# Layer 3 of a four-layer graph network: exponentiated logits used untransposed, with column maxima spread over DRAM and subtracted on GpSimd

## The chip, the cores and the metric

The kernel runs on one core of a Trainium2 chip. The metric is the device time of one execution in microseconds (us); the times are the median of the runs of each kernel. The profile is one execution taken by the hardware profiler.

## What is computed

`x` has shape (32, 512, 64): 32 graphs of 512 nodes with 64 features each; `adj` is one symmetric 512 x 512 matrix with the diagonal in it and few other edges, scaled on both sides by node degrees. Four layers follow each other, each with a layer norm and a ReLU ahead of it and a residual sum behind it. The first two are plain graph convolutions, the third is graph attention. The fourth, called layer 3 in the code, is the one that is changed:

```python
def gat_layer(x, graph, W, b):
    h = x @ W
    s = jnp.einsum('bnd,bmd->bnm', h, h) * graph
    s = jnp.where(s == 0.0, NEG_INF, s)
    a = jax.nn.softmax(s, axis=2)
    return jnp.einsum('bnm,bmd->bnd', a, h) + b
heads = jax.vmap(lambda W, b: gat_layer(flow_x, graph, W, b))(Wh, bh)
...
x = jax.nn.leaky_relu(cat, negative_slope=0.01)
out = gat_layer(x, graph, W_out, b_out)
return jax.nn.leaky_relu(out, negative_slope=0.01)
```

There are 8 heads of width 128, their outputs are concatenated, and one more attention of width 64 (`W_out`) works on them. The logits of a graph and head are a product of `h` with itself, so that `s` is symmetric: s[n, m] = s[m, n] wherever `graph` is.

## The kernel before

The kernel has two forms. `fast_form` is the one that runs: it relies on properties of the inputs (each diagonal entry present, the matrix being a degree scaling of its own pattern, no logit exactly zero on an edge), checks them while it works, and sets a flag; `general_form` is run afterwards if the flag is set. All data are fp32. Layers 0 to 2 make stage 1, about the first 455 us, in which layer by layer and pair of graphs by pair of graphs are interleaved by hand. Layer 3 takes the rest.

**Units.** The work of layer 3 is cut into 144 units: 128 `Heads` units (a graph b and two heads, `k` = 0 and 1) and 16 `Out` units (the output attention of two graphs, `k` = 0 and 1). A unit has C = 4 row blocks of P = 128 nodes. All units go through the same steps, and `planned` (line 690) writes the order of the work out by hand: in each `slot` k it issues, for every unit, the step whose offset from the unit's start (4 slots a unit) is due. In these slots TensorE, VectorE and ScalarE run strictly in the written order (`manual_schedule`); GpSimd and SyncE (SP), which only issue DMAs, were left to the scheduler.

**Steps of a unit**, with offsets in slots from its start:
- -1 to 2, `scores` (line 387): two TensorE products (k = 0, 1; each uses one half of the array's rows) put 128 x 512 logits for each k into PSUM (`s_ps`, two buffers).
- 0 to 3, `soft` (line 363): for each k one VectorE instruction (line 378) reads the logits, adds the mask `flow_neg` (SBUF), writes the negated logits to `s_att` in SBUF and leaves the negated row maximum in `negmax`; then ScalarE computes the exponential with the row maximum as bias (line 371) and sums the row.
- The value product needs the exponentials with the *other* node index on the partitions, so that they are transposed. For column blocks 0 to 2, `transpose` (line 422) makes 16 TensorE transposes of 64 x 64 (line 430) and copies the result from PSUM by ScalarE (lines 436, 438) or VectorE (line 441). For the last column block, `turn` (line 397, slots 2 to 5) transposes 32 x 32 blocks on VectorE (line 401), sends them to DRAM (line 406), and `route` (line 411) brings them back in transposed order (line 415).
- VA = 6 to 9, `values` (line 443): the value products add into `av` in PSUM (line 452; each k has one half of the array's columns).
- 5, `recips` (line 458): reciprocals of the row sums, transposed and sent over DRAM, come back spread over the partitions as `recb` (lines 463 to 473).
- END = 9, `normalize` (line 480): VectorE multiplies `av` by `recb` into `o_att` (line 482).
- 10, `row_halves` of a Heads unit (line 538): the two products y with the heads' weights (line 565), bias on ScalarE (line 573) into `cat`; in 11 VectorE's leaky ReLU on `cat`, 1024 elements a partition (`leaky`, line 312). An Out unit has a bias, a leaky ReLU, transposes back, the residual sum (line 651) and the store.

Beside these steps, every second Heads unit makes `g` for two units (line 547), every fourth one the layer norm of its graph on VectorE (lines 513 to 522, four instructions), and an Out unit's product with `W_out` (line 604) is spread over 8 slots, one head a slot. Out units are put into the list behind the heads of their graphs; those of the last few pairs are kept back for the end (`LATE` = 3).

Of the kernel before, what the change touches and what calls it, by code (L numbers as in the profile page):

```python
# [22 lines left out]
def fast_form(  # L23
# [169 lines left out]
    def judge_rows(c):  # L193
        edge, t = row_pair("edge"), row_pair("t")[:, 0]
        ok, edge = edge[:, 1], edge[:, 0]
# [9 lines left out]
        nc.vector.tensor_reduce(sound[:, 2 + C + c : 3 + C + c], ok, AX.X, OP.min)  # L205
# [4 lines left out]
    def row_pair(name):  # L210

        return early.tile([P, 2, N], F32, name=name, tag="row", bufs=H + 3)


    acc_of = []
# [46 lines left out]
    def flow_weights():  # L262
        whT = early.tile([P, H, 2, F], F32, name="whT", tag="row", bufs=H + 3)
# [36 lines left out]
    TR = C + 1  # L300
    VA = TR + 1
    END = VA + C - 1


    LATE = 3

    recs = [const.tile([P, 32], F32, name=f"rec{i}") for i in range(2)]
    for rec in recs:
        nc.gpsimd.memset(rec, 0.0)
# [4 lines left out]
    class Pair:  # L314
# [4 lines left out]

        def begin(self):
            self.p = pbuf.tile([P, 2, C, N], F32, name="p_att")
            self.sum = tiny.tile([P, 2, C], F32, name="sum_att")
            self.negmax = tiny.tile([P, 2, C], F32, name="negmax")
            self.pts = {}

# [7 lines left out]

# [5 lines left out]


# [13 lines left out]
        def scores(self, r):  # L360
            pass

        def soft(self, r, mid):

            if r == 0:
                self.begin()
            ps = self.s_ps.pop(r)
            ns = wk.tile([P, 2, N], F32, name="s_att", bufs=3)

            def exp(k):  # L370
                nc.scalar.activation(  # L371
                    self.p[:, k, r, :], ns[:, k], AF.Exp,
                    bias=self.negmax[:, k, r : r + 1], scale=-1.0,
                    accum_out=self.sum[:, k, r : r + 1],
                )

            for k in range(2):
                nc.vector.tensor_tensor_reduce(  # L378
                    out=ns[:, k], in0=ps[:, k], in1=flow_neg[:, r], scale=-1.0, scalar=BIG,
                    op0=OP.add, op1=OP.min, accum_out=self.negmax[:, k, r : r + 1],  # L380
                )
                if k == 0:
                    exp(0)
            mid()
            return lambda: exp(1)

        def scores(self, r):
            g, x = self.terms()
            ps = ps_s.tile([P, 2, N], F32, name="s_ps")
            self.s_ps[r] = ps  # L390
            for k in range(2):
                nc.tensor.matmul(  # L392
                    ps[:, k], lhsT=g[halves(k), r * P : (r + 1) * P], rhs=x[halves(k), :],
                    start=True, stop=True,
                )

        def turn(self, r):
            if r == 0:
                self.turns = wk.tile([P, Q, C // 2, 2, 2, 32], F32, name="turn")
                self.rows = dram.tile([P, Q, C // 2, P], F32, name="turn_row")  # L400
            nc.vector.transpose(  # L401
                self.turns[:, :, r // 2, :, r % 2].rearrange("p a k i -> p k a i"),
                self.p[:, :, r, N - P :].rearrange("p k (a i) -> p k a i", i=32),
            )
            if r % 2:
                nc.gpsimd.dma_start(  # L406
                    self.rows[:, :, r // 2],
                    self.turns[:, :, r // 2].rearrange("p a k r i -> p a (k r i)"),
                )

        def route(self):
            rows = self.rows.rearrange("(b i) a g x -> a i b (g x)", b=Q)
            pt = wk.tile([P, Q, C // 2, 2, 2, 32], F32, name="turned")
            for a in range(Q):
                (nc.sync if a % 2 else nc.gpsimd).dma_start(  # L415
                    pt[a * 32 : (a + 1) * 32].rearrange("p b g k r i -> p b (g k r i)"), rows[a]
                )
            self.pts[C - 1] = [
                pt[:, :, :, k].rearrange("p b g r i -> p g r b i") for k in range(2)
            ]  # L420

        def transpose(self, j):
            pt = pbuf.tile([P, 2, N], F32, name="pt_att", bufs=2)
            self.pts[j] = [pt[:, k] for k in range(2)]

            ps = [ps_m.tile([P, 2, C, F], F32, name="pt_ps", tag="m") for half in range(2)]
            for k in range(2):
                for r in range(C):
                    for half in range(2):
                        nc.tensor.transpose(  # L430
                            ps[half][:, k, r],
                            self.p[halves(half), k, r, j * P : (j + 1) * P],
                            ident[halves(half), halves(half)],
                        )
            pth = pt.rearrange("p k (r half q) -> p k r half q", r=C, half=2)
            nc.scalar.copy(pth[:, :, :, 0, :], ps[0])  # L436
            if j != 1:
                nc.scalar.copy(pth[:, :, :, 1, :], ps[1])  # L438
                return None
# [1389 lines left out]
```

## Time and profile before

| | before |
|---|---|
| median of 3 runs | 2256.88 us (2256.71 to 2257.84) |
| profiled execution | span 2255.2 us (from its first to its last instruction; no other time was recorded for it) |
| TensorE busy (PE) | 2181.2 us, 97% |
| VectorE busy (DVE) | 1746.9 us, 77% |
| ScalarE busy (ACT) | 1629.8 us, 72% |
| GpSimd busy (POOL) | 399.5 us, 18% |
| first and last instruction of line 378 | 454.2 and 2228.4 us |
| steady stretch 700 to 2100 us | PE 1372.7, DVE 1086.4, ACT 1143.3, POOL 289.9 us busy; granted TensorE clock 1.00 |

How such lines are read: a group's line has the source line, the engine, the operation, the tile it writes and those it reads, their shapes, the number of instructions, then the busy time in all and the mean in ns of one, then how long the engine stood idle just before them and what ended most of that. PEld is the loading of weights, which overlaps products. A fp32 product is issued as two instructions, so that a pair of products (k = 0 and 1) shows as x4. A row of waits reads "who, line <- whom, line: us in total, times, longest". A row in order of time has the start, the duration, and the instruction. The busy time of TensorE counts pipelined products, whose ends are modelled, so that full is not the same as at its peak; distances from start to start are the better measure.

### The profile page before, as it was taken

The numbers are of one execution on the slowest core, as the hardware profiler recorded it, in microseconds if no ns is written. First come the engines' busy times: TensorE is split into PE (matmuls) and PEld (weight loads), VectorE is DVE, ScalarE is ACT, GpSimd is POOL, SyncE is SP. The second block draws the span as 40 slices with busy tenths as digits, with TensorE's granted clock in tenths as the row PEclk, the third lists the DMA queues.
The fourth block names the chain that finished last, engine by engine and source line by source line (L and its number), as shares of the span: only waits on it lengthen the run. The fifth ranks groups of instructions, "written<-read, shape, count | busy, mean of one in ns | idle before, by whom it ended". The sixth has DMA issues, their size and how long they took to land.

```text
span 2255.2 us, 47785 instructions
## 1 busy us (share of the span) xinstructions
PE 2181.2 (97%) x17374; PEld 1032.9 (46%) x17374; DVE 1746.9 (77%) x4541; ACT 1629.8 (72%) x3815; POOL 399.5 (18%) x616
## 2 busy tenths in 40 slices
PE   7999999999999999999999999999999999999997
PEld 4667666634444444444444434444444443434443
DVE  6799986687778787878777777787878787878785
ACT  3444443288888888878888888787878787878785
POOL 2000000012121222222221212221212222212221
PEclk9999999899999999999999999999999999999999
DMA  4000000033333333333333333333333333333333
GB/s 130 1 1 1 1 1 1 1 93 113 104 115 105 113 109 112 110 106 111 109 110 112 110 107 114 104 114 108 116 102 118 102 115 107 106 99 117 99 115 105
DMA packets 122979, 204.03 MB, mean 90 GB/s; under 512 B 29752, under 2 KB 76000, under 8 KB 122608
## 3 DMA queue, kind: packets, MB, share of 16 engines
q0 software_dynamic: 37376, 113.49, 16.5%
q1 hardware_dynamic: 85360, 87.42, 13.0%
q8 instruction: 139, 2.28, 0.4%
q14 instruction: 104, 0.85, 0.1%
HBM read 119.48 MB, written 80.28 MB: 89 GB/s over the span
## 4 chain that ended last, share of the span: by engine, by line
PE 76%; DVE 17%; issue 3%; DMA 2%; ACT 1%; SPq 0%; DVEq 0%; ACTq 0%
PE s_ps L392 19%; PE av L452 18%; PE pt_ps L430 8%; DVE s_att L378 8%; PE nt_ps L880 7%; PE acc L972 5%; PE y_ps L565 5%; PE gT_ps L604 5%; DVE pt_att L441 3%; PE g_ps L547 2%; PE po L899 1%; DVE hs L518 1%; DVE turn L401 1%; PE wh_ps L925 1%; PE po1a L899 1%
## 5 line engine op out<-in xcount | busy, mean ns | idle before, releaser
L371 ACT ACTIVATE p_att<-s_att,negmax 128x512 f32<-128x512 f32 x1152 | 826.9, 726 | 1.8 <-DVE negmax L378 0.8
L378 DVE CUSTOM_DVE_ANT_0 s_att<-s_ps,flow_neg 128x512 f32<-128x512 f32 x1152 | 736.6, 675 | 1.7 <-PE s_ps L392 1.6
L392 PE MATMUL s_ps<-hx,g 64*128 64x512 f32 x2048 | 571.8, 635 | 26.4 <-DVE negmax L378 23.1
L452 PE MATMUL av<-pt_att,hn 128*64 128x512 f32 x1536 | 414.2, 618 | 0.0
L406 POOL DMA_DIRECT2D turn_row<-turn x288 | 206.3, 716 | 1161.8 <-DVE turn L401 970.6
L430 PEld LDWEIGHTS pt_ps<-ident,p_att 64*128 64x128 f32 x6912 | 279.7, 138 | 280.3 <-issue 180.0
L436 ACT COPY pt_att<-pt_ps 128x512 f32<-128x512 f32 x432 | 250.7, 580 | 88.9 <-PE pt_ps L430 86.8
L430 PE MATMUL pt_ps<-ident,p_att 64*128 64x64 f32 x6912 | 312.8, 226 | 1.2 <-ACT pt_att L436 0.6
L392 PEld LDWEIGHTS s_ps<-hx,g 64*128 64x128 f32 x2048 | 155.2, 186 | 282.9 <-DVE negmax L378 129.1
L401 DVE STREAM_TRANSPOSE turn<-p_att 128x256 f32<-128x256 f32 x576 | 254.0, 441 | 18.1 <-ACT p_att L371 17.6
L573 ACT ACTIVATE cat<-y_ps,bh 128x512 f32<-128x512 f32 x256 | 162.0, 684 | 132.3 <-PE y_ps L565 132.3
L482 DVE TENSOR_TENSOR o_att<-av,recb 128x512 f32<-128x512 f32 x144 | 99.5, 691 | 190.4 <-PE av L452 177.6
L441 DVE COPY pt_att<-pt_ps 128x512 f32<-128x512 f32 x144 | 99.0, 688 | 180.9 <-PE pt_ps L430 180.9
L415 POOL DMA_DIRECT2D turned<-turn_row x288 | 163.1, 573 | 390.9 <-DMA turn_row<-turn 205.8
L371 ACT ACTIVATION_READ_ACCUMULATOR p_att<-s_att,negmax 128x1 f32 x1152 | 229.5, 199 | 0.0
L438 ACT COPY pt_att<-pt_ps 128x512 f32<-128x512 f32 x288 | 171.5, 596 | 0.0
L452 PEld LDWEIGHTS av<-pt_att,hn 128*64 128x64 f32 x1536 | 75.9, 134 | 193.7 <-issue 81.9
L312 DVE SCALAR_TENSOR_TENSOR cat<-cat 128x1024 f32<-128x1024 f32 x128 | 151.4, 1183 | 0.0
L452 PE MATMUL av<-turned,hn 128*64 128x256 f32 x1024 | 139.6, 392 | 0.5 <-DMA turned<-turn_row 0.5
L559 ACT COPY g<-g_ps 128x512 f32<-128x512 f32 x128 | 68.7, 589 | 91.7 <-PE g_ps L547 91.7
L565 PE MATMUL y_ps<-o_att,wh_sb 64*128 64x512 f32 x512 | 132.9, 596 | 0.8 <-DVE o_att L482 0.8
L604 PE MATMUL gT_ps<-cat,wo_sb 128*64 128x512 f32 x512 | 131.9, 592 | 0.0
(176 smaller groups left out, 2165.0 us busy)
## 6 DMA issues: line engine op xcount, KB each, us to landing
turn_row<-turn POOLq DMA_DIRECT2D x288, 256.0 KB, 2.7
turned<-turn_row SPq DMA_DIRECT2D x288, 128.0 KB
turned<-turn_row POOLq DMA_DIRECT2D x288, 128.0 KB, 3.0
recb<-rec_row SPq DMA_DIRECT2D x288, 128.0 KB
rec_row<-rect SPq DMA_DIRECT2D x576, 1.0 KB
out_dram<-y SPq DMA_DIRECT2D x32, 128.0 KB
x<-in_x_dram SPq DMA_DIRECT2D x3, 1024.0 KB
x<-in_x_dram SPq DMA_DIRECT2D x4, 256.0 KB
```

Of the source, the lines that this page charges most:

```text
L371: nc.scalar.activation(self.p[:, k, r, :], ns[:, k], AF.Exp, bias=self.negmax[:, k, r : r + 1], scale=-1.0, accum_out=self.sum[:, k, r : r ...
L378: nc.vector.tensor_tensor_reduce(out=ns[:, k], in0=ps[:, k], in1=flow_neg[:, r], scale=-1.0, scalar=BIG, op0=OP.add, op1=OP.min, accum_out ...
L392: nc.tensor.matmul(ps[:, k], lhsT=g[halves(k), r * P : (r + 1) * P], rhs=x[halves(k), :], start=True, stop=True,)
L401: nc.vector.transpose(self.turns[:, :, r // 2, :, r % 2].rearrange("p a k i -> p k a i"), self.p[:, :, r, N - P :].rearrange("p k (a i) -> ...
L406: nc.gpsimd.dma_start(self.rows[:, :, r // 2], self.turns[:, :, r // 2].rearrange("p a k r i -> p a (k r i)"),)
L430: nc.tensor.transpose(ps[half][:, k, r], self.p[halves(half), k, r, j * P : (j + 1) * P], ident[halves(half), halves(half)],)
L436: nc.scalar.copy(pth[:, :, :, 0, :], ps[0])
L438: nc.scalar.copy(pth[:, :, :, 1, :], ps[1])
L441: return lambda: nc.vector.tensor_copy(pth[:, :, :, 1, :], ps[1])
L452: nc.tensor.matmul(self.av[halves(k), g * n : (g + 1) * n], lhsT=self.v(k, j), rhs=pt[k][:, g] if parts > 1 else pt[k], start=(j == 0), st ...
L565: nc.tensor.matmul(ps, lhsT=wh_sb[halves(k), h, :], rhs=self.o[halves(k), :], start=True, stop=True,)
L604: nc.tensor.matmul(self.gps[halves(k), :], lhsT=wo_sb[:, h, :], rhs=Heads.cat[b + k, h], start=(h == 0), stop=(h == H - 1),)
```

## The change

Because the logits are symmetric, the exponentials with the maximum of their *column* subtracted, in the layout in which they are computed, are the transposed softmax numerators with the row maximum subtracted. So the transposes go, and the maxima, which are found one for each partition, have to be spread along the free dimension:

- `maxima` (slots 0 to 3) is the VectorE instruction of line 378, which now writes the negated logits straight into `p` (one tile of 128 x 2 x 512 for each row block, 13 buffers) and the row maxima into one 128 x 32 tile.
- `spread_out` (slot 3) transposes that tile on VectorE and writes it to DRAM by four DMAs; `spread_in` (slot 4) reads it back to all 128 partitions as `topb`, 128 x 1024.
- `shift` (slots 7 to 10) subtracts `topb` from `p` on GpSimd, 1024 elements a partition; `exps` (8 to 11) is one ScalarE exponential of 1024 elements, in place; `values` (9 to 12) takes `p` itself.
- The sums are now over partitions: `tally` (slots 10 and 12) adds two row blocks on VectorE, twice a unit; `totals` (13) multiplies the two results by a 128 x 32 tile of ones on TensorE, four products, each on 32 columns; ScalarE copies them to SBUF. `totals_out` (14, four DMAs), `totals_in` (15), `recips` (17, an add and a reciprocal on VectorE, one DMA), `recips_in` (18, two DMAs) bring the reciprocals to `recb`.
- `park` (12) copies `av` to SBUF on ScalarE; `normalize` (END = 20) multiplies it by `recb` there.
- y, the bias and the leaky ReLU follow in slot 22, all in the same slot. `LATE` is 6, and Out units come 6 units behind the heads.
- All DMAs of layer 3 are issued by SP, and SP and GpSimd run in the written order, too.
- In stage 1 `judge_rows` also checks that the pattern of edges is symmetric: one more VectorE instruction, and a reduction of 1024 instead of 512 elements, four times.
- The pool of `cat` and similar tiles is split in one for stage 1 and one of 9 buffers for layer 3.

```diff
-        nc.vector.tensor_reduce(sound[:, 2 + C + c : 3 + C + c], ok, AX.X, OP.min)
+        nc.vector.scalar_tensor_tensor(
+            edge, adj_t[:, c], 0.0, edge, op0=OP.not_equal, op1=OP.is_equal
+        )
+        nc.vector.tensor_reduce(
+            sound[:, 2 + C + c : 3 + C + c], both.rearrange("p k n -> p (k n)"), AX.X, OP.min
+        )
...
-    TR = C + 1
-    VA = TR + 1
-    END = VA + C - 1
-    LATE = 3
+    SUB = 7
+    EX = SUB + 1
+    VA = EX + 1
+    PARK = VA + C - 1
+    TOT = PARK + 1
+    INV = TOT + 4
+    END = INV + 3
+    LATE = 6
+    ROOM = END // C + 2
...
-        def soft(self, r, mid):
-        def turn(self, r):
-        def route(self):
-        def transpose(self, j):
+        def maxima(self, r):
             if r == 0:
+                self.begin()
+            ps = self.s_ps.pop(r)
+            self.p[r] = pbuf.tile([P, 2, N], F32, name="p_att")
+            for k in range(2):
+                at = k * C + r
+                nc.vector.tensor_tensor_reduce(
+                    out=self.p[r][:, k], in0=ps[:, k], in1=flow_neg[:, r], scale=-1.0,
+                    scalar=BIG, op0=OP.add, op1=OP.min, accum_out=self.top[:, at : at + 1],
+                )
+
+        def spread_out(self):
+            t = tiny.tile([P, 32], F32, name="top_t")
+            nc.vector.transpose(t, self.top)
+            self.top_row = dram.tile([2 * C, P], F32, name="top_row")
+            for q in range(Q):
+                nc.sync.dma_start(
+                    self.top_row[:, q * 32 : (q + 1) * 32], t[q * 32 : q * 32 + 2 * C, :]
+                )
+
+        def spread_in(self):
+            self.topb = wk.tile([P, 2, N], F32, name="topb")
+            nc.sync.dma_start(
+                self.topb.rearrange("p k n -> p (k n)"),
+                self.top_row.rearrange("(o r) p -> o (r p)", o=1).to_broadcast([P, 2 * N]),
             )
+
+        def shift(self, r):
+            nc.gpsimd.tensor_tensor(self.p[r], self.p[r], self.topb, OP.subtract)
+
+        def exps(self, r):
+            nc.scalar.activation(self.p[r], self.p[r], AF.Exp, scale=-1.0)
 
         def values(self, j):
-            pt = self.pts.pop(j)
             if j == 0:
                 self.av = ps_v.tile([P, N], F32, name="av")
             for k in range(2):
+                nc.tensor.matmul(
+                    self.av[halves(k), :], lhsT=self.v(k, j), rhs=self.p[j][:, k],
+                    start=(j == 0), stop=(j == C - 1),
+                )
+
+        def tally(self, half):
+            a, b = self.p[2 * half], self.p[2 * half + 1]
+            nc.vector.tensor_tensor(a, a, b, OP.add)
+
+        def park(self):
+            self.o = wk.tile([P, N], F32, name="o_att", bufs=4)
+            nc.scalar.copy(self.o, self.av)
+
+        def totals(self):
+            ps = ps_m.tile([P, N], F32, name="tot_ps", tag="m")
+            for k in range(2):
+                for half in range(2):
+                    q = (2 * k + half) * 32
                     nc.tensor.matmul(
+                        ps[q : q + 32, :], lhsT=ones, rhs=self.p[2 * half][:, k],
+                        start=True, stop=True,
+                    )
+            self.tot = wk.tile([P, N], F32, name="tot")
+            nc.scalar.copy(self.tot, ps)
+
+        def totals_out(self):
+            self.tot_row = dram.tile([Q, N], F32, name="tot_row")
+            for q in range(Q):
+                nc.sync.dma_start(self.tot_row[q : q + 1, :], self.tot[q * 32 : q * 32 + 1, :])
+
+        def totals_in(self):
+            self.parts = tiny.tile([P, 2, 2, C], F32, name="parts")
+            nc.sync.dma_start(
+                self.parts.rearrange("p k h r -> p (k h) r"),
+                self.tot_row.rearrange("q (p r) -> p q r", r=C),
+            )
 
         def recips(self):
+            rec = tiny.tile([P, 2, C], F32, name="rec_flow")
+            nc.vector.tensor_tensor(rec, self.parts[:, :, 0], self.parts[:, :, 1], OP.add)
+            nc.vector.reciprocal(rec, rec)
+            self.rec_row = dram.tile([2, N], F32, name="rec_row")
+            nc.sync.dma_start(self.rec_row.rearrange("k (p r) -> p k r", r=C), rec)
+
+        def recips_in(self):
             self.recb = wk.tile([P, N], F32, name="recb")
             for k in range(2):
                 nc.sync.dma_start(
+                    self.recb[halves(k), :], self.rec_row[k : k + 1].to_broadcast([F, N])
                 )
 
         def normalize(self):
-            self.o = wk.tile([P, N], F32, name="o_att")
-            nc.vector.tensor_tensor(self.o, self.av, self.recb, OP.mult)
+            nc.vector.tensor_tensor(self.o, self.o, self.recb, OP.mult)
...
-            return off == END + 1 or off == -C and self.i % 2 == 0
+            return off == END + 2 or off == -C and self.i % 2 == 0
...
             for u, r in at(k, -1):
                 u.scores(r)
+            for u, r in at(k, SUB):
+                u.shift(r)
+            for u, r in at(k, EX):
+                u.exps(r)
+            for u, off in list(led_in(k)):
                 u.row_halves(off)
             for u, j in at(k, VA):
                 u.values(j)
...
+            for u, j in at(k, TOT, 1):
+                u.totals()
             for u, j in at(k, END, 5):
                 u.end_pe(j)
+            for u, j in at(k, PARK, 1):
+                u.park()
+            for u, j in at(k, C, 1):
+                u.spread_in()
+            for u, j in at(k, TOT + 1, 1):
+                u.totals_out()
+            for u, j in at(k, TOT + 2, 1):
+                u.totals_in()
+            for u, j in at(k, INV + 1, 1):
+                u.recips_in()
+            for u, r in at(k, 0):
+                u.maxima(r)
+            for u, j in at(k, C - 1, 1):
+                u.spread_out()
+            for u, j in at(k, -2, 1):
+                u.make_gs()
+            for u, j in at(k, INV, 1):
+                u.recips()
+            for u, j in at(k, END, 1):
+                u.normalize()
+            for off, half in ((EX + 2, 0), (EX + 4, 1)):
+                for u, j in at(k, off, 1):
+                    u.tally(half)
             for u, j in at(k, END, 5):
                 u.end_late(j)
...
+    pbuf = ctx.enter_context(tc.tile_pool(name="pbuf", bufs=3 * C + 1))
...
+            mybir.EngineType.Pool,
+            mybir.EngineType.SP,
```

## The prediction

> **What bounds the kernel now.** I read the page first, then the busy times of the steady middle (700 to 2100 us of the span), then its waits, then one unit in order of time.
>
> ```profile
> PE 2181.2 (97%) x17374; PEld 1032.9 (46%) x17374; DVE 1746.9 (77%) x4541; ACT 1629.8 (72%) x3815; POOL 399.5 (18%) x616
> PE 76%; DVE 17%; issue 3%; DMA 2%; ACT 1%; SPq 0%; DVEq 0%; ACTq 0%
> L378 DVE CUSTOM_DVE_ANT_0 s_att<-s_ps,flow_neg 128x512 f32<-128x512 f32 x1152 | 736.6, 675 | 1.7 <-PE s_ps L392 1.6
> L430 PE MATMUL pt_ps<-ident,p_att 64*128 64x64 f32 x6912 | 312.8, 226 | 1.2 <-ACT pt_att L436 0.6
> L312 DVE SCALAR_TENSOR_TENSOR cat<-cat 128x1024 f32<-128x1024 f32 x128 | 151.4, 1183 | 0.0
> ```
>
> TensorE is nearly full and carries 76% of the chain that ended last. Layer 3 is 144 units of 4 slots (128 Heads, 16 Out). Line 378 runs 904 times in the 1400 us of the middle, twice a slot: 452 slots, 3.10 us each, **12.39 us a unit**. The next rows show how TensorE fills it:
>
> ```profile
> 1003.29 1.03 PE L604 MATMUL gT_ps<-cat,wo_sb 128*64 128x512 f32 x4
> 1004.25 1.13 PE L392 MATMUL s_ps<-hx,g 64*128 64x512 f32 x4
> 1005.22 0.66 PE L430 MATMUL pt_ps<-ident,p_att 64*128 64x64 f32 x16
> 1005.80 1.09 PE L452 MATMUL av<-turned,hn 128*64 128x256 f32 x8
> 1006.72 1.03 PE L604 MATMUL gT_ps<-cat,wo_sb 128*64 128x512 f32 x4
> ```
>
> From start to start, a pair of 512-column products (two halves of the array at once) takes 0.95 us, a group of 16 transposes about 0.62. A Heads unit has 4 score pairs, 4 value pairs, 1 pair y, half a pair g, about 0.9 of Out's products: 10.4 x 0.95 = 9.9, plus 3 x 0.62 = 1.9 of transposes, 0.15 for hx: 11.9 of 12.39 us. The rest is short waits:
>
> ```profile
> PEld s_ps L392 <- DVE negmax L378: 125.2, 135, 1.4
> DVE o_att L482 <- PE av L452: 140.5, 109, 2.4
> ```
>
> VectorE waits for TensorE about as often as TensorE for it. GpSimd only issues DMAs in this stage. Its one elementwise kind is in stage 1:
>
> ```profile
> L1047 POOL TENSOR_TENSOR x<-x,bias_b 128x512 f32<-128x512 f32 x16 | 20.4, 1277 | 280.0 <-DVE hn L822 280.0
> 313.31 1.27 DVE L858 TENSOR_REDUCE var<-sq 128x8 f32<-128x512 f32 x2
> ```
>
> The second row is what VectorE does beside the GpSimd add that starts at 313.47: a reduction with one SBUF input, in each place that I looked at. The trace never shows a GpSimd elementwise instruction beside a VectorE instruction that reads two SBUF tensors, which is what the change brings in.
>
> [...]
>
> **The change, part by part, per unit.**
>
> *TensorE.* Out: three groups of transposes, -1.9 us. In: four ones products, each 32 columns wide. Lower bound 0.95 if all four overlap; upper 4 x 0.95 = 3.8 if none does; I take 0.95, as the 64-wide pairs overlap fully. Value products of the last block become ordinary ones (same time). Sum 11.0 us.
>
> *ScalarE.* Out: 8 exps (issue distance 0.71) and 5 copies (0.48), -8.1 us. In: 4 exps of 1024 (between 0.73 and 2 x 0.71; 1.15 taken), two copies 1.0. Off the path either way, about 7.5 us.
>
> *VectorE, issue distances.* 8 maxima x 0.61 = 4.85; spread-out transpose 0.2; recips 0.4; normalize 0.61; cat's leaky 1.10 (line 312); two tallies of 1024, like line 312, 1.15 each; the norm of every fourth unit 1.84/4 = 0.46. Sum **9.9 us**; the transposes of 0.44 and the copy of 0.69 that go are replaced by the tallies.
>
> *GpSimd.* DMA issues out; four shifts, 9.4 us, in. Alone it would fit.
>
> *SP.* 13 DMAs a unit in written order, issue 0.3 to 0.5 us each, 5.1 in all. It must wait for the landing of the spread maxima, the totals and the reciprocals: rec_row's last issue to recb is 2.3 us (1010.55 to 1012.87), so about 5 us more: some 10 us. Behind a waiting DMA stand the other units' DMAs, and behind those Pool's shift and VectorE's recips and normalize; each has two or three slots of lead, so I cost it at nothing beyond the first; with no lead a landing would cost 2.3.
>
> *The p buffers.* 13 for tiles that live up to 14 slots. Totals free two of four tiles, tallies free the other two earlier, so a free one exists: nothing (upper bound 1.6 us, two maxima and the hand-over, if maxima had to wait for the totals of their own slot).
>
> *cat and leaky now in the same slot.* y is TensorE's second pair of its slot: 1.9 us plus 0.2, then ScalarE's two activations of 0.63: leaky starts 3.4 us after the slot and ends at 4.5, the next maxima at 5.8. TensorE wants them at 4.75: about 1.1 us of stall.
>
> *The shared reads.* Both tallies, leaky, normalize (it now reads SBUF twice), recips and the norm read two SBUF tensors, 5.0 us a unit. Cost between nothing (no exclusion) and 2.35 x 5 = 11.8 (each meets a whole shift). I follow one unit with exclusion, 0 at TensorE's start of the slot with y. Topb lands 7.4 us after the fourth maxima (0.2 transpose, 1.3 issue, 2.2 landing, 0.5 issue, 3 landing as for turned), so shifts start at 0.85. First shift to 3.2; tally (asked at 1.55) to 4.35; second shift to 6.7, while leaky (asked at 4.4) waits, then to 7.8; maxima to 9.05 and 10.45, third shift 7.8 to 10.15, fourth to 12.5; normalize (asked at 10.45) to 13.1; tally to 14.25; maxima to 15.5, TensorE's next start 15.6. TensorE, with 11.0 us of work, waits. VectorE waits 1.65 + 2.3 + 2.05 = 6.0: 9.5 + 6.0 + hand-over = 15.6 for a unit without norm. A unit with norm adds 1.84 and another meeting or two, on average +0.5: **16.1 us**.
>
> *Outside the units.* The four judged rows of stage 1 gain a product and a longer reduction, 4 x 1.25 = 5 us on VectorE, 80% busy there: 0 to 5, 3 taken. The tail: from the last maxima to the end it was 19.6 us (2229.0 to 2248.6); now spread 7.2, shifts 9.4, exp, values, tally and totals 3.4, out and back of the totals 7.6, reciprocals out and back 6.6, the end 5.5: about 40. +20. SP and GpSimd in written order as well: no more.
>
> Sum against the profiled span of 2255.2: 144 x (16.1 - 12.39) = +534, +20, +3: 2812. The median of the runs (2256.9) is 1.7 above: **2814 us**.
>
> **The rivals.** (1) *Nothing excludes* and the change is faster. The same walk without port waits is bound by TensorE with leaky's stall: 11.0 + 0.7 (half of the stall hides behind product slots) = 11.7 us, 144 x -0.69 = -99, +23: 2180. For it: TensorE bounds now, and the removed transposes are on its chain. Against: [...] VectorE is left only 2 us of slack. The point from which it decides: port waits under about 0.5 us a unit; above that the gain is gone. (2) *Partial slowing*: the two take turns finely and a shared 5 us is stretched, or SP's landings bind: about 13 us a unit, 2255 + 88 + 23 = 2368. [...] (3) *Pool saturates*: shifts and VectorE's shared reads back to back, 9.4 + 5.0 = 14.4 us: 2255 + 289 + 23 = 2568, the lower end of my case. (4) Totals that don't overlap: 13.9 us on TensorE, hidden under 16.1, but 2490 if nothing excludes. (5) If maxima too were excluded (they read PSUM and SBUF), 19 us, 3230[...]. That the flag sends the program to the general form: no sign of it, below 1%.
>
> **How the numbers follow.** Exclusion with 14.4 to 17.2 us a unit (2568 to 2975): 0.72, likeliest 2814. Partial or SP-bound, (2) and (4): 0.10. Faster, (1): 0.15. Rest 0.03. Leaving out (1) and the far end gives 2240 to 2980. A difference under 0.2% is what cannot be told from none: 0.02. Faster 0.16, slower 0.82.
>
> **What would show it.** Right: VectorE instances of the tally, normalize and leaky that last 1.2 to 3.5 us or start late with nothing else due, 15 to 17 us between units, s_ps waiting for VectorE's maxima, TensorE under 75% busy, shifts near 2.35 us. The totals: four within about 1 us. The prediction is wrong if tallies keep 1.2 us beside a running shift, or if topb or recb are what VectorE and GpSimd wait for.

## The result and the profile after

| | before | after |
|---|---|---|
| median | 2256.88 us | 2847.81 us (2833.47 to 2855.13, 4 runs) |
| ratio to before | | 1.261, 95% interval 1.257 to 1.265: slower |
| span of the profiled execution | 2255.2 us | 2831.7 us |
| first and last maxima | 454.2, 2228.4 us | 453.3, 2779.4 us |
| a unit: (last - first) / 144 | 12.32 us | 16.15 us |
| granted TensorE clock, mean of the span | 0.992 | 0.905 |

Of the 576.5 us between the spans, 552 lie in the units (144 x 3.83), 25.5 between the last maxima and the end of the span (52.3 against 26.8), and -0.9 ahead of the first maxima. These are the page's busy times and costliest groups of the kernel after (the columns are those of before):

```profile
PE 2289.4 (81%) x11038; PEld 801.4 (28%) x11038; DVE 2483.9 (88%) x4257; ACT 1166.2 (41%) x1655; POOL 1649.6 (58%) x617
...
L398 POOL TENSOR_TENSOR p_att<-p_att,topb 128x1024 f32<-128x1024 f32 x576 | 1619.6, 2842 | 863.6 <-DMA topb<-top_row 618.5
L376 DVE CUSTOM_DVE_ANT_0 p_att<-s_ps,flow_neg 128x512 f32<-128x512 f32 x1152 | 735.9, 675 | 74.1 <-PE s_ps L364 73.8
...
L401 ACT ACTIVATE p_att<-p_att 128x1024 f32<-128x1024 f32 x576 | 595.9, 1058 | 9.4 <-POOL p_att L398 9.3
...
L414 DVE TENSOR_TENSOR p_att<-p_att 128x1024 f32<-128x1024 f32 x288 | 527.9, 1833 | 2.9 <-ACT p_att L401 2.9
L323 DVE SCALAR_TENSOR_TENSOR cat<-cat 128x1024 f32<-128x1024 f32 x128 | 342.6, 2677 | 113.8 <-ACT cat L545 113.8
...
L459 DVE TENSOR_TENSOR o_att<-o_att,recb 128x512 f32<-128x512 f32 x144 | 253.0, 1757 | 6.5 <-DMA recb<-rec_row 6.5
```

TensorE's busy share fell and VectorE's rose, although VectorE has hardly more to compute: it was busy for 9.6 us a unit before, and for 10.0 in experiment 1 below, where nothing is stretched. The leaky ReLU (L323) is the same instruction as L312 of before, where it took 1183 ns; now the mean is 2677. The normalize (L459) went from 691 to 1757 ns; before, it read `av` from PSUM:

```profile
L482 DVE TENSOR_TENSOR o_att<-av,recb 128x512 f32<-128x512 f32 x144 | 99.5, 691 | 190.4 <-PE av L452 177.6
```

The maxima, which read PSUM and SBUF, keep their 675 ns to the nanosecond. This points away from what these instructions do and to whom they meet; the experiments test it. The chain of the page breaks off after some 4% of the span and is no help here; the waits of the steady stretch (900 to 2500 us, 98.9 units) are:

```profile
PEld s_ps L364 <- DVE top L376: 321.9, 199, 7.1
POOL p_att L398 <- DMA topb<-top_row: 311.6, 55, 9.8
...
DVE cat L323 <- ACT cat L545: 83.6, 63, 2.8
```

TensorE's weight loads wait 3.3 us a unit for the maxima; before, 125.2 us in a stretch of 113 units, 1.1. GpSimd waits for the spread maxima, but nobody waits for GpSimd to that extent: ScalarE's exponentials, which follow the shifts, wait 9.3 us for them in the whole run (L401 above). VectorE's own list holds cat (0.85 us a unit), s_ps (0.5) and an Out unit's bias (0.1), 1.5 us a unit together. What VectorE loses otherwise is *inside* its instructions, where a list of waits doesn't show it. In order of time, VectorE's instructions of one unit, a product group of TensorE, and GpSimd's shifts:

```profile
1505.06 2.52 DVE L459 TENSOR_TENSOR o_att<-o_att,recb 128x512 f32<-128x512 f32 x1
1507.51 1.21 DVE L414 TENSOR_TENSOR p_att<-p_att 128x1024 f32<-128x1024 f32 x1
1508.64 0.68 DVE L376 CUSTOM_DVE_ANT_0 p_att<-s_ps,flow_neg 128x512 f32<-128x512 f32 x1
...
1511.35 2.20 DVE L414 TENSOR_TENSOR p_att<-p_att 128x1024 f32<-128x1024 f32 x1
1513.93 2.94 DVE L323 SCALAR_TENSOR_TENSOR cat<-cat 128x1024 f32<-128x1024 f32 x1 [0.38 <-ACT cat L545]
...
1509.61 1.07 PE L425 MATMUL tot_ps<-p_att,ones 128*32 128x512 f32 x8
...
1495.73 11.30 POOL L398 TENSOR_TENSOR p_att<-p_att,topb 128x1024 f32<-128x1024 f32 x4 [9.58 <-DMA topb<-top_row]
1510.09 11.33 POOL L398 TENSOR_TENSOR p_att<-p_att,topb 128x1024 f32<-128x1024 f32 x4 [3.06 <-DVE rec_flow L446]
```

Four shifts run from 1495.7 to 1507.0. The normalize at 1505.06 takes 2.52 us: it is issued during the last of them and ends 0.55 us after it. The tally behind it finds GpSimd idle and takes its own 1.21. From 1510.1 on the next four shifts run, of which the first two end at 1512.47 and 1515.78: the tally at 1511.35 has 2.20 us and ends 1.08 after the first, and leaky, issued behind it, has 2.94 and ends 1.09 after the second. All eight instructions of the totals (four products) start within one group that lasts 1.00 us from start to start (the next group starts at 1510.61), so the four 32-wide products together take about as long as the two 64-wide ones of y behind the next scores (L537, 0.96 us): they overlap.

The groups of the same stretch, with the alone time taken from those that met nobody (1209 ns for the tally, 1226 for leaky, 686 for the normalize, 414 and 423 for the norm), give the waiting inside the instructions. The prediction calls it port waits, and so it is called from here on; the runs show these waits, not what in the chip makes them:

```profile
L414 DVE TENSOR_TENSOR p_att<-p_att 128x1024 f32<-128x1024 f32 x198 | 353.3, 1784 | 0.0
L323 DVE SCALAR_TENSOR_TENSOR cat<-cat 128x1024 f32<-128x1024 f32 x92 | 245.9, 2672 | 83.6 <-ACT cat L545 83.6
L459 DVE TENSOR_TENSOR o_att<-o_att,recb 128x512 f32<-128x512 f32 x99 | 180.7, 1826 | 0.0
...
L485 DVE TENSOR_TENSOR hn<-x,mean 128x256 f32<-128x256 f32 x23 | 54.2, 2355 | 0.0
L486 DVE SCALAR_TENSOR_TENSOR hn<-hn,rstd 128x256 f32<-128x256 f32 x22 | 49.7, 2261 | 0.8
```

198 x 0.575 + 92 x 1.446 + 99 x 1.140 + 23 x 1.94 + 22 x 1.84 = 114 + 133 + 113 + 45 + 40 = 445 us, 4.5 us a unit; smaller ones (an Out unit's leaky ReLU and `gs`, the sum in `recips`) add 0.2, so that the port waits come to **4.7 us a unit**. With VectorE's own 10.0 and its 1.5 of idle time this is the whole unit of 16.2 us in this stretch.

### The profile page after: what moved, and what is told of

It is laid out like the page before. It is cut to its first block, busy times and chain, and to the rows that moved or that the text cites. A ratio compares the mean times of both kernels' runs of the same rounds, so it can differ in the third digit from the quotient of the medians.

```text
span 2831.7 us, 33279 instructions
## 1 busy us (share of the span) xinstructions
PE 2289.4 (81%) x11038; PEld 801.4 (28%) x11038; DVE 2483.9 (88%) x4257; ACT 1166.2 (41%) x1655; POOL 1649.6 (58%) x617
## 5 line engine op out<-in xcount | busy, mean ns | idle before, releaser
L398 POOL TENSOR_TENSOR p_att<-p_att,topb 128x1024 f32<-128x1024 f32 x576 | 1619.6, 2842 | 863.6 <-DMA topb<-top_row 618.5
L376 DVE CUSTOM_DVE_ANT_0 p_att<-s_ps,flow_neg 128x512 f32<-128x512 f32 x1152 | 735.9, 675 | 74.1 <-PE s_ps L364 73.8
L401 ACT ACTIVATE p_att<-p_att 128x1024 f32<-128x1024 f32 x576 | 595.9, 1058 | 9.4 <-POOL p_att L398 9.3
L407 PE MATMUL av<-p_att,hn 128*64 128x512 f32 x2048 | 585.7, 652 | 2.0 <-ACT p_att L401 2.0
L414 DVE TENSOR_TENSOR p_att<-p_att 128x1024 f32<-128x1024 f32 x288 | 527.9, 1833 | 2.9 <-ACT p_att L401 2.9
L323 DVE SCALAR_TENSOR_TENSOR cat<-cat 128x1024 f32<-128x1024 f32 x128 | 342.6, 2677 | 113.8 <-ACT cat L545 113.8
L459 DVE TENSOR_TENSOR o_att<-o_att,recb 128x512 f32<-128x512 f32 x144 | 253.0, 1757 | 6.5 <-DMA recb<-rec_row 6.5
L407 PEld LDWEIGHTS av<-p_att,hn 128*64 128x64 f32 x2048 | 106.3, 142 | 441.5 <-issue 173.2
L425 PE MATMUL tot_ps<-p_att,ones 128*32 128x512 f32 x1152 | 182.3, 605 | 7.5 <-DVE p_att L414 7.5
L537 PE MATMUL y_ps<-o_att,wh_sb 64*128 64x512 f32 x512 | 131.2, 589 | 0.0
L934 PE MATMUL acc<-v,s 64*128 64x65 f32 x2048 | 124.3, 280 | 0.7 <-DVE s L920 0.4
```

The source lines that it names most:

```text
L323: nc.vector.scalar_tensor_tensor(t, t, 0.01, t, op0=OP.mult, op1=OP.max)
L376: nc.vector.tensor_tensor_reduce(out=self.p[r][:, k], in0=ps[:, k], in1=flow_neg[:, r], scale=-1.0, scalar=BIG, op0=OP.add, op1=OP.min, ac ...
L398: nc.gpsimd.tensor_tensor(self.p[r], self.p[r], self.topb, OP.subtract)
L401: nc.scalar.activation(self.p[r], self.p[r], AF.Exp, scale=-1.0)
L407: nc.tensor.matmul(self.av[halves(k), :], lhsT=self.v(k, j), rhs=self.p[j][:, k], start=(j == 0), stop=(j == C - 1),)
L414: nc.vector.tensor_tensor(a, a, b, OP.add)
```

## The experiments

The theory is that of the prediction: GpSimd's shift and a VectorE instruction that reads two SBUF tensors exclude each other for whole instructions. The rivals are that TensorE's new order, the place of leaky, the landings or GpSimd's mere activity cost it. All edits are against the kernel after unless said otherwise; "a unit" is (last - first maxima) / 144 of the profiled run.

**1. No shifts** (e1).

```diff
-            nc.gpsimd.tensor_tensor(self.p[r], self.p[r], self.topb, OP.subtract)
+            pass
-            nc.scalar.activation(self.p[r], self.p[r], AF.Exp, scale=-1.0)
+            nc.scalar.activation(self.p[r], self.p[r], AF.Exp, scale=-1e-6)
```

> Leaves out the subtraction of the column maxima (no GpSimd instruction in layer 3), and scales the logits by 1e-6 in the exponential, so that they stay finite; all else, the spread of the maxima over DRAM too, is as in the changed kernel. Theory (VectorE and GpSimd exclude each other on shared reads): tally back to 1.2, cat's leaky to 1.2, normalize to 0.7 us, 11.3 to 12.2 us a unit, 2130 to 2260 us. Rival (waits for landings in written order, or leaky in the same slot, hold the units): above 2500 us, VectorE waiting for recb or for cat.

Measured: 2295.16 us (2293.17 to 2296.94), ratio 1.017 [1.015, 1.019]; 12.44 us a unit. VectorE's groups between 900 and 2100 us:

```profile
L414 DVE TENSOR_TENSOR p_att<-p_att 128x1024 f32<-128x1024 f32 x190 | 231.6, 1219 | 0.0
L323 DVE SCALAR_TENSOR_TENSOR cat<-cat 128x1024 f32<-128x1024 f32 x88 | 107.9, 1226 | 205.3 <-ACT cat L545 205.3
```

All stretched instructions are back at their own time, and 553 of the 591 us are gone, although TensorE's order, leaky's place and the landings stay as they are: the shifts are the cause. But it is 38 us *slower* than before, where 2130 to 2260 us were expected. Leaky now waits in its slot for ScalarE, 2.3 us in each of 88 units, with the maxima queued behind it. This is a second fault, in the kernel after hidden in part behind the first (0.85 us a unit of waiting for cat).

**2. The pairs by themselves** (e2): GpSimd and VectorE each run a list of instructions on tiles of 128 x 1024 fp32, alone and beside each other; the kernel computes nothing of the layers and ran once.

> Computes nothing of the reference: it copies x to the output and measures instructions of 128x1024 fp32 on GpSimd and VectorE, first alone, then side by side. Theory: GpSimd's two-input subtraction alone 2.35 us; beside it a VectorE add of two SBUF tensors takes 1.2 us plus up to 2.35 of waiting, a VectorE add of PSUM and SBUF and a reduction keep their time, and an add beside a GpSimd fill (which reads nothing) keeps its time, too. With two GpSimd instructions of 512 in place of one of 1024 the wait is at most 1.3 us. Rival (bandwidth shared finely): both slow down in every pairing with two SBUF inputs by the same factor, whatever the length of GpSimd's instruction.

In order of time: first subtractions alone (L33), two-SBUF additions alone (L42), a copy alone (L51); then the pairs.

```profile
22.28 9.23 POOL L33 TENSOR_TENSOR g<-in_a,in_b 128x1024 f32<-128x1024 f32 x4
41.72 4.62 DVE L42 TENSOR_TENSOR v<-in_c,in_d 128x1024 f32<-128x1024 f32 x4
52.17 2.49 DVE L51 COPY v<-in_e 128x1024 f32<-128x1024 f32 x4
60.69 38.41 POOL L33 TENSOR_TENSOR g<-in_a,in_b 128x1024 f32<-128x1024 f32 x12
60.84 52.96 DVE L42 TENSOR_TENSOR v<-in_c,in_d 128x1024 f32<-128x1024 f32 x24
114.34 52.80 DVE L42 TENSOR_TENSOR v<-in_c,in_d 128x1024 f32<-128x1024 f32 x24
167.68 27.33 DVE L42 TENSOR_TENSOR v<-in_c,in_d 128x1024 f32<-128x1024 f32 x24
200.13 27.72 POOL L33 TENSOR_TENSOR g<-in_a,in_b 128x1024 f32<-128x1024 f32 x12
200.29 27.23 DVE L48 TENSOR_TENSOR v<-ps,in_d 128x1024 f32<-128x1024 f32 x24
228.40 30.06 DVE L45 TENSOR_REDUCE stat<-in_e 128x1 f32<-128x1024 f32 x24
258.84 32.54 POOL L33 TENSOR_TENSOR g<-in_a,in_b 128x1024 f32<-128x1024 f32 x12
258.99 40.17 DVE L51 COPY v<-in_e 128x1024 f32<-128x1024 f32 x24
```

Alone a subtraction takes 9.23 / 4 = 2.31 us and an addition 4.62 / 4 = 1.155. Beside each other, 12 subtractions run for 38.41 us and the first 12 additions for about as long; the other 12 additions follow in 13.7 us, at their own time. From the second on, starts lie 3.28 us apart on both engines: they alternate one to one, and a pair takes 3.28 us against a sum of 3.43 (alone, from start to start, 2.30 and 1.13). Next (114.34) the subtractions are halves, 24 of them, which alone take 1.22: 52.8 / 24 = 2.20 a pair, against a sum of 2.35. That is turns of whole instructions with an overlap of some 0.15 us; if both shared finely, the length of GpSimd's instruction would make no difference to an addition, which takes 3.35 us beside whole subtractions and 2.28 beside halves. Three neighbours are harmless: GpSimd fills, which only write (167.68: 24 additions in 27.33 us, 1.14 each), an addition with one input in PSUM (200.29: 24 in 27.23 us, 1.13 each, and 12 subtractions in 27.72, 2.31 each), and a reduction (228.40: 1.25 each, alone 1.24). A plain copy from SBUF to SBUF is not, although it has one input: starts lie 2.75 us apart on both engines against a sum of 2.90, and the other 12 copies follow in 7.3 us. Why the copy takes turns with a subtraction and the reduction does not, no run shows.

**3. GpSimd as busy, but only writing** (e7).

```diff
-            nc.gpsimd.tensor_tensor(self.p[r], self.p[r], self.topb, OP.subtract)
+            blank = wk.tile([P, 448], F32, name="blank", bufs=1)
+            for _ in range(6):
+                nc.gpsimd.memset(blank, 0.0)
```

and the exponential's scale as in 1.

> As e1, but GpSimd fills a scratch tile of 448 six times where the shift was (about 2.5 us of work that reads nothing in SBUF; the maxima are not subtracted, logits scaled by 1e-6). Theory (exclusion needs reads on both sides): as e1, 2255 to 2335 us. Rival (a busy GpSimd as such, or its place in the order, slows VectorE): 2500 us or more.

Measured: 2298.37 us (2297.26 to 2299.93), ratio 1.018 [1.017, 1.020], where no shifts at all gave 1.017 [1.015, 1.019]. GpSimd was busy for 1070 of 1200 us, more than in the kernel after (833 us of the same stretch). A busy GpSimd costs 3 us at most; its reads of SBUF are what costs the rest.

**4. Leaky one slot later** (e4), **5. the same without shifts** (e5).

```diff
-            if step == 2:
+            if step == 3:
                 leaky(self.cat)
```

> cat's leaky ReLU one slot later than y, as in the kernel before. Theory: the idle time of VectorE before it (0.84 us a unit) goes, the port waits stay: 2690 to 2830 us. Rival (the same-slot wait is what costs): 2600 us or less.

> As e1 (no subtraction of the column maxima, logits scaled by 1e-6 in the exponential), and cat's leaky ReLU one slot later than y. Theory (without exclusion the wait for cat in its own slot is what was left, 2.3 us of VectorE's time a unit in e1): TensorE bounds again, 11.3 to 11.7 us a unit, 2165 us (2110 to 2230), faster than before. Rival (the landings on SP, or the p tiles, hold the units at 12.6 us): 2270 to 2310 us, as e1.

| median, us | leaky in the slot of y | one slot later | the slot |
|---|---|---|---|
| with shifts | 2847.81 | 2641.59 (2640.32 to 2644.26) | 206 |
| without | 2295.16 | 2169.47 (2169.25 to 2170.32) | 126 |
| the shifts | 553 | 472 | |

The ratios of the right column to before are 1.171 [1.169, 1.173] and 0.962 [0.960, 0.963]. The second is what was expected; the first lies between its two expectations. With shifts, what goes is VectorE's idle time: 1.5 us a unit in the kernel after, 0.3 now, as the waits for s_ps and in the Out units shrink with the one for cat, which the expectation counted alone. The port waits are still there, 4.6 us a unit against 4.7, but they have moved. Leaky no longer follows a tally, and its mean falls from 2677 to 1765 ns; the tallies rise to 2048, and the small sum in `recips` (L446), 210 in the kernel after, to 1022:

```profile
L414 DVE TENSOR_TENSOR p_att<-p_att 128x1024 f32<-128x1024 f32 x162 | 331.8, 2048 | 0.0
L323 DVE SCALAR_TENSOR_TENSOR cat<-cat 128x1024 f32<-128x1024 f32 x73 | 128.8, 1765 | 5.4 <-ACT cat L545 5.4
...
L446 DVE TENSOR_TENSOR rec_flow<-parts 128x8 f32<-128x8 f32 x81 | 82.8, 1022 | 0.0
```

Of the second kernel, TensorE's products:

```profile
1500.92 1.13 PE L364 MATMUL s_ps<-hx,g 64*128 64x512 f32 x4
1501.98 1.08 PE L407 MATMUL av<-p_att,hn 128*64 128x512 f32 x4
1502.99 1.13 PE L364 MATMUL s_ps<-hx,g 64*128 64x512 f32 x4
```

TensorE is busy for 1182 of 1200 us there, so that this is its own pace: 11.58 us a unit. Where score and value pairs take turns, they take 1.06 + 1.01 us from start to start, not 2 x 0.95.

**6. Shifts in halves** (e3).

```diff
-            nc.gpsimd.tensor_tensor(self.p[r], self.p[r], self.topb, OP.subtract)
+            for k in range(2):
+                nc.gpsimd.tensor_tensor(self.p[r][:, k], self.p[r][:, k], self.topb[:, k], OP.subtract)
```

> Each shift is cut into two GpSimd instructions of 512. Theory (held for a whole instruction): each meeting costs at most 1.28 instead of 2.35 us, so that about half of the 4.7 us of waiting a unit goes: 13.9 us a unit, 2530 us (2450 to 2650), though GpSimd works longer (10.2 instead of 9.4 us). Rival (shared finely): no gain, 2830 to 2950 us.

Measured: 2674.34 us (2671.48 to 2685.45), ratio 1.185 [1.183, 1.187]; 15.12 us a unit. If VectorE is held off for a whole instruction of GpSimd's, a shorter one must cost it less at each meeting, and it does: 173 us less although GpSimd's work grows by 6% (1.23 x 2 against 2.31). It gains less than expected (2450 to 2650): the tally's mean is still 2000 ns, leaky's 2000, the normalize's 1316, and the port waits only fall from 4.7 to 3.9 us a unit. VectorE loses less at each meeting (the normalize 0.77 us in place of 1.81, leaky 0.83 in place of 1.55, the tally 0.96 in place of 1.28), but meets more often: 81% of the tallies and 79% of the normalizes are stretched by over 0.1 us, where in the kernel after 49% and 59% are.

**7. Leaky with one input in PSUM** (e8): ScalarE writes 0.01 y (`bh01` is 0.01 times the bias), and VectorE takes the maximum of y in PSUM and this; **8. the same one slot later** (e11).

```diff
-                        self.cat[:, k], pss[k], AF.Identity, bias=bh[:, h : h + 1], scale=1.0
+                        self.cat[:, k], pss[k], AF.Identity, bias=bh01[:, h : h + 1], scale=0.01
...
-                leaky(self.cat)
+                for k in range(2):
+                    h = 2 * self.i + k
+                    nc.vector.scalar_tensor_tensor(
+                        self.cat[:, k], self.y[k], bh[:, h : h + 1], self.cat[:, k],
+                        op0=OP.add, op1=OP.max,
+                    )
```

> The full computation; of the changed kernel only cat's leaky ReLU is other: it reads y from PSUM beside 0.01 y from SBUF, so that it has one SBUF input, in the same slot. Theory: its 1.5 us of port wait a unit goes, the wait for cat stays: 14.9 us a unit, 2670 us (2600 to 2760). Rival (its place in the slot costs[...]): 2780 us or more.

> As e8, and one slot later than y [...]. Theory: against e4 (2642 us) the leaky's remaining wait of 0.55 us a unit goes: 2560 us (2480 to 2640). Rival: no gain over e4.

Measured: 2654.24 us (2652.38 to 2667.64), ratio 1.178 [1.175, 1.181], and 2586.85 us (2584.32 to 2589.42), 1.146 [1.145, 1.148]. Both lie in the range of the theory. The mean of leaky's halves is 742 and 728 ns. What remains is the tally, at 2070 and 2118 ns, and the normalize. The port waits are 3.8 and 3.9 us a unit: of the 1.35 us that leaky no longer waits, the tallies and `recips` take up a part.

**9. No tally either** (e9), **10. with leaky one slot later** (e10): beside the edit of 7, eight ones products of the raw numerators take the place of four of their sums, one slot earlier.

```diff
-            nc.vector.tensor_tensor(a, a, b, OP.add)
+            pass
...
-                    nc.tensor.matmul(
-                        ps[q : q + 32, :], lhsT=ones, rhs=self.p[2 * half][:, k],
-                        start=True, stop=True,
-                    )
+                    for i in range(2):
+                        nc.tensor.matmul(
+                            ps[q : q + 32, :], lhsT=ones, rhs=self.p[2 * half + i][:, k],
+                            start=(i == 0), stop=(i == 1),
+                        )
...
-            for u, j in at(k, TOT, 1):
+            for u, j in at(k, TOT - 1, 1):
```

> The full computation. No tally: the ones products take all four row blocks (8 products in place of 4, one slot earlier), and cat's leaky ReLU reads y from PSUM on VectorE beside 0.01 y from SBUF, so that it has one SBUF input. Left of the two-input instructions: normalize, recips and the norm. Theory: 12.6 us a unit, 2320 us (2260 to 2420). Rival (GpSimd itself or the landings bound it): 2600 us or more.

> As e9, with cat's leaky ReLU one slot later than y. Theory: the wait for cat goes, too, TensorE (12.0 us of products a unit) bounds: 12.2 to 12.5 us, 2275 us (2230 to 2340), about the kernel before. Rival: no gain over e9.

Measured: 2610.77 us (2603.28 to 2617.21), 1.157 [1.154, 1.160], and 2509.66 us (2500.11 to 2516.65), 1.112 [1.109, 1.116]. Both lie above the ranges of their theory, by 190 and 170 us; the first is within its rival's (GpSimd or the landings bound it), the second gains 101 us over the first, where its rival had no gain. The port waits are down to 2.1 and 2.3 us a unit. VectorE has a wait that the kernel after doesn't have; in the second one, between 900 and 2100 us:

```profile
DVE p_att L378 <- PE tot_ps L428: 260.0, 82, 5.9
```

Maxima wait for a p tile, as all four of a unit now live until the totals. That looked like what held them.

**11. A fourteenth p tile** (e12), against 10; two other tiles get one buffer to make room.

```diff
-    pbuf = ctx.enter_context(tc.tile_pool(name="pbuf", bufs=3 * C + 1))
+    pbuf = ctx.enter_context(tc.tile_pool(name="pbuf", bufs=3 * C + 2))
```

> As e10 with one more tile for p (14 in place of 13; the room comes from one tile each for the totals and for recb in place of two). In e10 VectorE stood idle 3 us a unit for the totals that free p tiles. Theory: that was what made e9 and e10 slower than expected; TensorE then bounds, 12.8 us a unit, 2350 us (2290 to 2420). Rival (TensorE was the bound of e10 already, at its lower granted clock, or GpSimd's remaining meetings were): 2480 us or more.

Measured: 2486.50 us (2481.31 to 2496.99), 1.102 [1.099, 1.106]. This is within the range of the rival, and the theory's is missed. The wait for a tile is gone, and another has its size, 279.8 us of s_ps: TensorE itself was late, with or without the tile. A unit with a norm shows one reason (VectorE, then TensorE):

```profile
1519.85 2.46 DVE L489 SCALAR_TENSOR_TENSOR hn<-hn,rstd 128x256 f32<-128x256 f32 x1
1522.35 2.72 DVE L493 TENSOR_TENSOR hs<-hn,root_d 128x512 f32<-128x512 f32 x1
...
1525.21 0.87 PE L298 MATMUL hx_ps<-ident,hs 128*128 128x128 f32 x4 [1.81 <-DVE hs L493]
1526.67 2.08 PE L366 MATMUL s_ps<-hx,g 64*128 64x512 f32 x4 [0.59 <-DVE top L378]
```

The norm's instructions stand in a row, need 0.42 and 0.69 us alone, and take 2.46 and 2.72 here. TensorE waits 1.81 us for them, and its next score pair takes 2.08 us in place of 1.13 (see the last section).

**12. The same without shifts** (e13): the edits of 11 and 1.

> The version with ones products in place of the tallies, leaky from PSUM one slot later and 14 p tiles, with the four shifts of a unit left out (the exponential gets a scale of -1e-6, so that every numerator is about 1 and no subtraction is done). Theory, [...] of that version's 14.0 us a unit, everything above TensorE's own 12.0 us comes from the normalize, the norm and the small sums that meet a shift, directly or through TensorE's pauses after them. Then without shifts a unit costs 12.0 to 12.3 us: 2165 to 2250, 2210 likeliest, and the TensorE clock is 0.98 or more. Rival, something in TensorE's own order (eight ones products, the p tiles, the copy of av) holds it as well: at least 13 us a unit, 2340 or more, with TensorE still waiting.

Measured: 2308.28 us (2307.93 to 2309.62), ratio 1.024 [1.022, 1.025]; 12.55 us a unit. It lies between the two expectations. Busy times (TensorE's is the first number after the length), then a wait, both of 900 to 2100 us:

```profile
900.00:2100.00 1200.00, 1172.12 (x5546) 323.45 (x5536) 764.01 (x2176) 643.08 (x874) 0.00 (x0) 1.00 0.23 66
```

```profile
DVE p_att L378 <- PE s_ps L366: 386.4, 256, 4.0
```

TensorE is full, and VectorE waits for it. 11.58 us of experiment 5 and 0.87 for the second set of ones products (from start to start 1.87 us for 16 instructions against 1.00 for 8) are 12.45, which explains the pace but for 0.1 us. So this repair can't reach the kernel before even if the subtraction were free. It cut what the shifts cost from 553 to 178 us (2486.5 - 2308.3), and paid for that with TensorE's time.

No version here that does the whole computation beats the kernel before. Experiment 5 would, but it leaves the subtraction out.

## Why the prediction was right, and where its terms were off

**The mechanism and the total.** 2814 us were forecast, 2847.81 measured. The forecast's main case, exclusion for whole instructions, was an assumption of the author's: no trace of before shows it. It is now shown from three sides: leaving the shifts out (1), the pair by itself (2), and a busy GpSimd that doesn't read (3). Whole-instruction turns are shown by the one-to-one alternation of 2 and by halves (6). The unit, 16.1 us forecast, is 16.15; the maxima, rival 5, are untouched. Neither the partial slowing of rival 2 nor rival 4 (totals apart) took place. One SBUF input alone decides nothing: the copy of experiment 2 has one and contends (2.75 us from start to start, 0.60 alone), the reduction has one and does not (1.25, alone 1.24). The kernel after has no such copy beside its shifts.

**Terms that held.** A shift alone: 2.35 us, a figure of the author's that the trace of before does not give (it has 1277 ns for 512 elements a partition); 2.31 in experiment 2, from start to start, at least 2.335 in the kernel. The totals: 0.95 and 1.00; a single 128-wide product of 512 columns takes 0.88 us in stage 1 of before (L880, four in 3.53 from 307.04 on), so that a pair in 0.95 and four in 1.00 do overlap. The p buffers at nothing: the kernel after has no wait for a p tile among VectorE's; they bind only in 9 and 10, where the tiles live longer. SP and the landings at nothing: the normalize waits 6.5 us for recb in the whole run; GpSimd does wait for topb, 311.6 us in 98.9 units, which the prediction named as a sign of being wrong; but it has time to spare there, as the exponentials wait only 9.3 us for it in the whole run.

**Terms of the unit that cancelled.** The port waits were put at 6.0 us, all of them in three meetings of about 2 us each, of a tally, of leaky and of the normalize. Those instructions wait 3.6 us (the tallies 1.15, leaky 1.35, the normalize 1.14): only 49% of the tallies and 59% of the normalizes meet a shift. For the norm 0.5 us a unit was added in all, but its own work, 1.84 / 4, is 0.46 of that, so that its meetings stood at next to nothing; they are 0.9. The small ones that were left out add 0.2. And VectorE is idle for 1.5 us, for which the sum had 0.1. So 4.7 + 1.5 stand where 6.0 + 0.1 stood, and with the 9.9 of VectorE's own work the sum comes out at 16.1 of 16.2 us. The mechanism was right; that the total came out within 1.2% is luck in part.

**Rival 1 had the wrong time.** It gave 11.7 us a unit and 2180 us if nothing excluded. Measured without exclusion: 12.44 and 2295. Both of its terms were small: TensorE's own pace is 11.58 us, not 11.0, mostly as the 8 score and value pairs of a unit take 1.01 us each on average in experiment 5, not 0.95 (+0.45); and leaky's slot costs 0.86, not 0.7. Its point of decision, port waits under 0.5 us a unit, was therefore wrong: with leaky in y's slot experiment 1 has none of these waits and gains nothing. The gain exists only one slot later (2169).

**The tail.** +20 us were forecast; by the same measure (end of the last maxima, 2780.1, to the end of the last sum, 2826.8) it is 46.7 us against 19.6, so +27. The last units' tallies take 3.35 to 3.37 us three times there and their normalize 2.17, meetings that the tail's sum left out. Stage 1, +3, comes out at -1 (453.3 against 454.2 for the first maxima): its longer checks are hidden.

**What was not foreseen at all** is TensorE's clock, 0.905. It is why one sign failed: TensorE was to be under 75% busy and is at 81%, as the same products take 12.9 us of its time a unit, against 11.5 in experiment 5. How much of the 16.15 us the clock holds was not tried apart; directly it can reach VectorE only through VectorE's idle time, 1.5 us a unit.

## What to carry to other kernels

Before work is moved to an idle GpSimd, count the VectorE instructions beside it that read two SBUF tensors: each may wait for a whole GpSimd instruction (the tally took 1.21 us alone, and up to 3.42 beside shifts of 2.34), and the profile books that as the instruction's own time, so that the sign to look for is a group whose mean lies above its minimum. Such instructions in a row can each wait anew (two of the norm's in 11: 2.46 and 2.72 us, 0.42 and 0.69 alone). A plain copy from SBUF to SBUF waited, too (2). Giving one input to PSUM took the wait off an instruction (7: leaky's mean from 2677 ns to two halves of 742), and shorter GpSimd instructions made each wait shorter (6: the normalize's from 1.81 to 0.77 us); but part of what one instruction gained, others lost, so the waits of all of them have to be added up. Moving one of them away from another (4) only moved the waits. And an edit that brings several things should be taken apart with the largest cost removed: what leaky's slot costs by itself, 126 us, could not be read beside the shifts, where moving it gave 206.

## What the runs showed of the hardware that was not expected

TensorE runs at about half its pace after two waits shown here, of 6.87 and 1.81 us. Of the kernel after, products around a stall of VectorE:

```profile
1560.72 1.08 PE L407 MATMUL av<-p_att,hn 128*64 128x512 f32 x4
1568.67 1.08 PE L296 MATMUL hx_ps<-ident,hs 128*128 128x128 f32 x4 [6.87 <-DVE hs L490]
1570.12 2.08 PE L364 MATMUL s_ps<-hx,g 64*128 64x512 f32 x4 [0.37 <-DVE top L376]
1571.99 1.92 PE L519 MATMUL g_ps<-hx,m 64*128 64x512 f32 x4
1573.84 1.22 PE L407 MATMUL av<-p_att,hn 128*64 128x512 f32 x4
1575.57 1.13 PE L364 MATMUL s_ps<-hx,g 64*128 64x512 f32 x4
```

After 6.87 us without work a pair takes 2.08 and 1.92 us, about twice its 1.13 and 1.03. The granted clock is 1.00 until some 2 us after the last product, 0.50 from 1564 on, and 1.00 again from 1574.2, 5.5 us after TensorE resumed. In layer 3 of this run it is at 0.50 in 82 stretches, 81 of them of 3.4, 6.8 or 10.2 us. The wait need not be so long: in experiment 11 (the unit shown there) TensorE waits 1.81 us, and its next pairs take 2.08, 1.91 and 1.97 us. Which waits slow it and which do not was not tried apart.

So a stall on another engine can cost more than its length (here 1.84 us more for the first two pairs behind it), and in these five runs the clock of the whole span falls with TensorE's busy share: it is 0.992 (before) and 0.988 (5) at 98% of the time between 900 and 2100 us, 0.962 (11) at 92%, 0.937 (4) at 85% and 0.905 (after) at 80%.
